# Right halves of four row tiles: two-by-two products of 256 features in place of full products of 512

## The chip, the core and the metric

The kernel runs on one core of a Trainium2 chip. The metric is device time in microseconds (us). Three runs of the kernel before took 358.38, 361.06 and 360.46 us, so the median is 360.46.

A core has a matrix engine (TensorE, PE in the profile), a vector engine (VectorE, DVE), a scalar engine (ScalarE, ACT), a general engine (GpSimd, POOL) and a queue engine that issues transfers (SyncE, SP). Each engine takes its own instructions in order and waits on semaphores for the others.

## The reference

Two layers follow each other on x of 2048 rows and 1024 features. Everything is float32.

```
attn = (w1.T @ w2.T) * sparse_mask                 # 1024 x 1024, a band and two stripes near it
y    = gelu(x @ attn + b2)
x    = layernorm(x + y)
w_l  = lut4[o, code of 4 bits], w_h = lut8[o, code of 8 bits]
y    = where(norm(x) > 64, x @ w_h.T, x @ w_l.T) + bias
x    = layernorm(x + y)
```

The first einsum multiplies each row of x by the masked product of the two weights. The rows of a normalized x have a norm near 32, so the kernel computes only the 4-bit case and counts the rows that would need the other; were there any, a general path would run behind it. It doesn't run with these inputs.

## The kernel before

**Tiles.** The rows are 16 tiles of 128 rows, and each x tile stays in SBUF. `attn` is kept as a band of at most 268 columns for each block of 128 input features. `attention(n)` copies the bias into a PSUM tile (ACT, L526), runs 10 matmuls with the transposed tile as the stationary side (L532), takes Gelu (ACT, L557), adds it to x with a row sum (DVE, L561), takes the sum of squares (ACT, `stats`, L380), r on POOL (L382, L383), and, later, the normalization (DVE, L387). The closures for the later step are kept in a list that `now()` works off.

**Second layer.** `wT` holds the 4-bit weights, transposed, as 8 blocks of 128 input features by 1024 output features; the identity is added to it, so x + y is one product. It is filled while the first tiles go through attention: ACT and POOL make table entries, DVE selects, TensorE transposes and ACT copies (L282). For tiles 0 to 3 (`EARLY`) the second layer is done in two halves of 512 output features: the left one (`ffn_half(n, xT, 0)`) while the weights of the right half are still being made, the right one later, between the attentions of tiles 12 to 15. A half is 8 matmuls of 512 columns (L575), an evacuation with a row sum (`combine`, L587), and at the end `finish_rows`.

**Pairs.** Tiles 4 to 15 go by twos through `ffn_pair`. It has Winograd's form of Strassen's scheme: with the two row tiles as the block rows, and the halves of input and of output features as block columns, seven products of four matmuls do for what is eight otherwise. It needs four weight sums T1 to T4 (`weight_sum`, L636, 128 x 2048 elements each: T1 = B12 - B11, T2 = B22 - T1, T3 = B22 - B12, T4 = B21 - T2) and sums of the transposed row tiles, s1 to s4 (`pair_inputs`: two on DVE, L675 and L676, two on POOL, L678 and L679). The transposed tiles for it are made by `squares`: a transpose of 32 x 32 squares on DVE (L642), a transfer to DRAM (`there`) and four back (`rows`). Products that are shared are accumulated in the same PSUM tile `u`, with DVE reading `u` in between (L705, L712 and `combine`), so TensorE has to wait for that reading before it goes on adding.

**Order.** The list `todo` gives the order in which the steps are written down. PE, ACT and POOL are then ordered by a scheduler with costs of its own. From attention of tile 8 on, DVE keeps the order in which the program is written (`manual_schedule` for DVE, L846). In the list, each right half `m` of 0 to 3 stands ahead of the attention of tile 12 + m, and the weight sum T(m + 1) stands right behind the right half. The pool `last` is opened ahead of tile 10 and takes over the room of the weight preparation, so what lies in it waits for that preparation to end.

Of the kernel before, what the change touches and what calls it, by code (L numbers as in the profile page):

```python
# [9 lines left out]
FP = mybir.dt.float32  # L10
# [22 lines left out]
EARLY = 4  # L33
# [159 lines left out]
def kernel(  # L193
# [21 lines left out]
    with ExitStack() as main:  # L215
# [330 lines left out]
        def now():  # L546
            while later:
                later.pop(0)()
# [24 lines left out]
        def product(ps, xT, h):  # L573
            for k in range(KT):
                nc.tensor.matmul(  # L575
                    out=ps,
                    lhsT=xT[:, k, :],
                    rhs=wT[:, k, ts(h, HALF)],
                    start=(k == 0),
                    stop=(k == KT - 1),  # L580
                )

        sums = const.tile([P, NT, NH], FP, name="sums")

        def combine(n, h, ps, other):

            return nc.vector.scalar_tensor_tensor(  # L587
                x_tiles[n][:, ts(h, HALF)],
                ps,
                1.0,  # L590
                other,
                ALU.mult,
                ALU.add,
                accum_out=sums[:, n, h : h + 1],
            )

        def finish_rows(n):
            y = x_tiles[n]
            total = work.tile([P, 1], FP, tag="total", name="total", bufs=4)
            nc.vector.tensor_tensor(total, sums[:, n, 0:1], sums[:, n, 1:2], ALU.add)  # L600
# [12 lines left out]
        def ffn_half(n, xT, h):  # L613
            ps = ps_mm.tile([P, D], FP, tag="mm", name="mm")
            product(ps[:, :HALF], xT, h)
            now()
            combine(n, h, ps[:, :HALF], bias_bc[:, ts(h, HALF)])
            if h == 1:
                finish_rows(n)

# [10 lines left out]
        def weight_sum(pool, i):  # L631

            plus, minus = sums_of[i]
            weights[i] = pool.tile([P, KH, HALF], FP, tag=f"t{i}", name=f"t{i}")
            minus = weights[minus] if isinstance(minus, int) else minus
            nc.vector.tensor_tensor(weights[i], plus, minus, ALU.subtract)  # L636

        def squares(pool, n):

# [18 lines left out]
        def pair_inputs(pool, n, top, low):  # L658


            def halves(tag):
                both = late.tile([P, KT, P], FP, tag=tag, name="halves")
                return both, both[:, :KH, :], both[:, KH:, :]

            def by_squares(block):
                return block.rearrange("p k (a r) -> p k a r", a=Q)


            side = (n - EARLY) // PAIR % 2
            (a1, a11, a12), (_, s1, s2), (_, s3, s4) = (  # L670
                halves(f"early{2 * i + side}") for i in range(3)
            )
            a22 = pool.tile([P, KH, P], FP, tag="a22", name="a22", bufs=2)
            nc.scalar.copy(by_squares(a1), top)  # L674
            nc.vector.tensor_tensor(by_squares(s1), low[:, :KH], low[:, KH:], ALU.add)  # L675
            nc.vector.tensor_tensor(by_squares(s3), top[:, :KH], low[:, :KH], ALU.subtract)  # L676
            copied = nc.scalar.copy(by_squares(a22), low[:, KH:])
            nc.gpsimd.tensor_tensor(s2, s1, a11, ALU.subtract)  # L678
            nc.gpsimd.tensor_tensor(s4, a12, s2, ALU.subtract)  # L679
            return (a11, a12, a22, s1, s2, s3, s4), copied  # L680

        def ffn_pair(pool, n, blocks, between):

            a11, a12, a22, s1, s2, s3, s4 = blocks
            t1, t2, t3, t4 = (weights[i] for i in range(1, 5))
            u = pool.tile([P, HALF], FP, tag="u", name="u", bufs=2)
            v = pool.tile([P, HALF], FP, tag="v", name="v", bufs=1)
            w = pool.tile([P, HALF], FP, tag="w", name="w", bufs=1)

            def times(ps, a, b, start, stop):  # L690
                for k in range(KH):
                    nc.tensor.matmul(  # L692
                        out=ps,
                        lhsT=a[:, k, :],
                        rhs=b[:, k, :],
                        start=start and k == 0,
                        stop=stop and k == KH - 1,
                        skip_group_check=True,
                    )
# [108 lines left out]
        for m in range(EARLY):  # L808
            todo += [("left", m), ("attention", 4 + m)]
        todo += [("attention", n) for n in range(4 + EARLY, SOON)]  # L810
        for m in range(EARLY):
            todo += [("right", m), ("attention", SOON + m)]
        unpack_after = [("attention", 1), ("left", 0), ("attention", 4), ("left", 1)]
        unpack_after += [("attention", 5), ("left", 2), ("attention", 6), ("left", 3)]

        kept = {}
        rows, blocks = {}, {}

        def prepare_pair(n, part):

# [12 lines left out]
        def prepare(what, n):  # L833
            if what == "attention":
                return first_xT[n] if n < AHEAD else transposed(n, "xT", 2, False)
            if what == "left":
                kept[n] = transposed(n, f"early{n}", 1, True)
            return kept[n]

        ready = prepare(*todo[0])  # L840
        ordered = main.enter_context(ExitStack())
        for i, (what, n) in enumerate(todo):
            if (what, n) == ("left", 0):
                transpose_pending(0)
            if (what, n) == ("attention", 2 * EARLY):
                ordered.enter_context(tc.manual_schedule(engines={mybir.EngineType.DVE}))  # L846
            if (what, n) == ("attention", SOON - 2):
                steps(100)
                transpose_pending(0)
                first_sb.close()  # L850
                last = main.enter_context(tc.tile_pool(name="last", bufs=1, side="right"))
                for m in range(SOON, NT):
                    load_x(last, m)
            xT = ready
            if i + 1 < len(todo):
                ready = prepare(*todo[i + 1])
            if what == "attention":
                if n >= SOON + 1:
                    attention(n, xT, lambda: prepare_pair(EARLY, n - SOON - 1))
                else:  # L860
                    attention(n, xT)
                if n < 2 * EARLY:
# [64 lines left out]
```

## Time and profile before

| what | us |
|---|---|
| median of three runs | 360.46 |
| profiled execution, its own time | 360.45 |
| its span in the profile | 358.7 |
| TensorE busy | 329.9 |
| VectorE busy | 214.5 |
| ScalarE busy | 179.4 |
| GpSimd busy | 90.9 |
| the chain that ended last: share of TensorE | 60% |
| DVE weight sum of 128 x 2048 (L636), each of four | 2.28 |
| POOL sum of 128 x 512 (L678, L679), mean | 1.585, 1.413 |

Times in the profile are counted from the start of the span. An instruction that waits is shown when it starts, with the idle time before it in brackets and what ended that. In the page's slices each digit is the busy share of one fortieth of the span in tenths. A float32 matmul is shown as two instructions, so eight matmuls are x16. The marks in time that the text uses: the four right halves lie between 157.0 and 201.5, the first pair begins at 201.5 and the second at 227.4.

### The profile page before, as it was taken

How to read it: one execution, taken by the hardware profiler on the slowest of the kernel's cores; microseconds unless marked ns; L12 is line 12 of the kernel's file. 1: busy time of each engine (PE TensorE's matmuls, PEld its weight loads, DVE VectorE, ACT ScalarE, POOL GpSimd, SP SyncE). 2: the span in 40 equal slices, each digit the busy share in tenths (PEclk: the TensorE clock that was granted, in tenths of full speed). 3: DMA queues.
4: the chain of work that ended last, by engine and by line, in shares of the span. 5: the costliest groups of instructions: out<-in, count | busy, mean ns of one | idle time of the engine just before them, and what ended most of it. 6: DMA issues, size and time to landing. Idle time of an engine off the chain costs nothing.

```text
span 358.7 us, 3719 instructions
## 1 busy us (share of the span) xinstructions
PE 329.9 (92%) x1228; PEld 205.7 (57%) x1228; DVE 214.5 (60%) x341; ACT 179.4 (50%) x257; POOL 90.9 (25%) x131
## 2 busy tenths in 40 slices
PE   7799867598999999999999998999999999999990
PEld 7688756495765759966656643443444443444450
DVE  0589898546997885436476853653644535634342
ACT  3795893978958988974346311303214114024020
POOL 1630431425013442312312530401304004004010
PEclk9899998879999999999999999999999999999996
DMA  8999207700000000320264425153554450441103
GB/s 250 320 320 384 80 0 288 298 2 0 0 0 2 1 0 3 126 111 26 79 215 165 140 80 175 58 199 100 199 177 137 188 175 8 189 154 58 58 3 125
DMA packets 28475, 43.90 MB, mean 122 GB/s; under 512 B 7584, under 2 KB 20640, under 8 KB 28448
## 3 DMA queue, kind: packets, MB, share of 16 engines
q1 hardware_dynamic: 26832, 42.66, 34.9%
q10 hardware_dynamic: 1616, 0.93, 0.9%
q8 instruction: 11, 0.18, 0.2%
q14 instruction: 16, 0.13, 0.1%
HBM read 28.90 MB, written 14.68 MB: 122 GB/s over the span
## 4 chain that ended last, share of the span: by engine, by line
PE 60%; ACT 12%; DMA 11%; DVE 8%; issue 3%; POOL 2%; SPq 2%; ACTq 0%; POOLq 0%; DVEq 0%
PE u L692 15%; PE mm L532 12%; PE mm L575 12%; PE w L692 8%; ACT e L322 6%; PE pt L281 5%; PE v L692 4%; PE mm L454 4%; DMA rows<-there 3%; ACT junk L380 2%; DMA q<-in_L_ffn_qweight_dram 2%; DMA x<-in_L_attn_x_dram 2%; DMA there<-squares 1%; DMA w_sb<-in_L_attn_w_dram 1%; SPq L652 1%
## 5 line engine op out<-in xcount | busy, mean ns | idle before, releaser
L532 PE MATMUL mm<-attn,xT 128*128 128x198 f32 (+2 forms) x320 | 62.5, 353 | 6.9 <-ACT mm L526 6.9
L380 ACT ACTIVATE junk<-x,nm 128x1024 bf16<-128x1024 f32 x31 | 35.7, 1151 | 59.7 <-DVE nm L377 57.3
L532 PEld LDWEIGHTS mm<-attn,xT 128*128 128x128 f32 x320 | 54.8, 197 | 14.6 <-ACT mm L526 7.6
L322 ACT ACTIVATE e<-v,lt,diff 128x1024 f32<-128x1024 uint8 x48 | 56.8, 1243 | 12.6 <-DVE v L297 11.0
L575 PE MATMUL mm<-wT,xT 128*128 128x512 f32 x128 | 56.4, 593 | 1.0 <-ACT wT L282 1.0
L326 POOL TENSOR_SCALAR root<-v,diff,lt 128x1024 f32<-128x1024 uint8 x16 | 31.3, 1965 | 57.9 <-DVE v L297 26.2
L692 PE MATMUL u<-t,halves 128*128 128x512 f32 x96 | 43.3, 593 | 1.0 <-DVE x L712 1.0
L575 PEld LDWEIGHTS mm<-wT,xT 128*128 128x128 f32 x128 | 23.7, 190 | 28.1 <-issue 26.1
L382 POOL TENSOR_SCALAR r<-ss 128x1 f32<-128x1 f32 x31 | 10.4, 334 | 108.8 <-ACT junk L380 108.6
L674 ACT COPY halves<-rows 128x1024 f32<-128x1024 f32 x6 | 6.3, 1048 | 55.4 <-DMA rows<-there 55.4
L454 PE MATMUL mm<-w2T,w_sb 128*128 128x268 f32 (+1 forms) x128 | 30.8, 391 | 2.2 <-ACT w2T L282 2.2
L692 PEld LDWEIGHTS u<-t,halves 128*128 128x128 f32 x96 | 18.2, 190 | 24.3 <-issue 22.5
L678 POOL TENSOR_TENSOR halves<-halves 128x512 f32<-128x512 f32 x6 | 9.5, 1585 | 84.5 <-DVE halves L675 68.3
L642 DVE STREAM_TRANSPOSE squares<-x 128x1024 f32<-128x1024 f32 x12 | 24.3, 2029 | 11.0 <-DMA there<-squares 11.0
L387 DVE TENSOR_SCALAR x<-x,nm,r 128x1024 f32<-128x1024 f32 x16 | 13.0, 813 | 29.0 <-POOL r L383 29.0
L330 DVE COPY_PREDICATED root<-v,e 128x1024 f32<-128x1024 uint8 x16 | 23.3, 1457 | 8.0 <-POOL root L326 4.6
L454 PEld LDWEIGHTS mm<-w2T,w_sb 128*128 128x128 f32 x128 | 23.8, 197 | 6.2 <-ACT w2T L282 2.7
L281 PE MATMUL pt<-ident,x 128*128 128x128 f32 x160 | 21.8, 281 | 4.0 <-DVE x L387 4.0
L561 DVE SCALAR_TENSOR_TENSOR x<-z,x 128x1024 f32<-128x1024 f32 x16 | 21.4, 1335 | 6.2 <-ACT z L557 6.2
L329 DVE COPY_PREDICATED e<-v,e 128x1024 f32<-128x1024 uint8 x16 | 21.3, 1329 | 3.5 <-ACT e L322 3.5
L281 PEld LDWEIGHTS pt<-ident,x 128*128 128x128 f32 x160 | 19.4, 152 | 5.9 <-DVE x L387 4.3
L282 ACT COPY xT<-pt 128x512 f32<-128x512 f32 x40 | 21.4, 591 | 2.3 <-PE pt L281 2.3
(93 smaller groups left out, 438.5 us busy)
## 6 DMA issues: line engine op xcount, KB each, us to landing
x<-in_L_attn_x_dram SPq DMA_DIRECT2D x16, 512.0 KB, 7.4
out_dram<-o SPq DMA_DIRECT2D x14, 512.0 KB, 2.6
there<-squares SPq DMA_DIRECT2D x12, 512.0 KB, 3.1
rows<-there SPq DMA_DIRECT2D x48, 128.0 KB, 2.9
w_raw<-in_L_attn_w_dram SPq DMA_DIRECT2D x8, 512.0 KB, 6.8
w_sb<-in_L_attn_w_dram SPq DMA_DIRECT2D x3, 1024.0 KB, 6.9
w_sb<-in_L_attn_w_dram SPq DMA_DIRECT2D x2, 512.0 KB, 7.2
x<-_L_attn_sparse_mask_dram SPq DMA_DIRECT2D x2, 413.0 KB, 3.7
```

Source lines behind the costliest of these rows:

```text
L281: nc.tensor.transpose(pt[:, j, :], block(g * (HALF // P) + j), ident)
L282: done = nc.scalar.copy(dst[:, g * (HALF // P) : (g + 1) * (HALF // P), :], pt)
L322: nc.scalar.activation(entry[j], plane(0), AF.Identity, scale=d_k, bias=l_k)
L326: nc.gpsimd.tensor_scalar(entry[j], plane(0), d_k, l_k, ALU.mult, ALU.add)
L330: nc.vector.copy_predicated(root, plane(1), entry[1])
L380: nc.scalar.activation(junk, u, AF.Square, bias=nm, accum_out=ss)
L454: part = nc.tensor.matmul(out=ps[:, : hi - lo], lhsT=w1_sb[s][:, k, :], rhs=w2T[:, k, lo:hi], start=(k == 0), stop=(k == KT - 1),)
L532: nc.tensor.matmul(out=ps[:, a:b], lhsT=xT[:, s, :], rhs=attn[:, s, a - lo : b - lo], start=False, stop=hi == D or (h == 0 and window(s + ...
L561: nc.vector.scalar_tensor_tensor(xt, z, 1.0, xt, ALU.mult, ALU.add, accum_out=total)
L575: nc.tensor.matmul(out=ps, lhsT=xT[:, k, :], rhs=wT[:, k, ts(h, HALF)], start=(k == 0), stop=(k == KT - 1),)
L642: nc.vector.transpose(out=t, in_=x_tiles[n].rearrange("t (c j k) -> t c k j", c=Q, k=KT))
L692: nc.tensor.matmul(out=ps, lhsT=a[:, k, :], rhs=b[:, k, :], start=start and k == 0, stop=stop and k == KH - 1, skip_group_check=True,)
```

## The change

The right halves of tiles 0 to 3 are no longer computed tile by tile. Tiles 0 and 1, and tiles 2 and 3, form a pair each, and the right half of 512 output features is cut in two of 256. So `ffn_rights` does seven products of four matmuls of 256 columns for two tiles; `u` and `w` take tiles of the transposes' PSUM pool, and `v` one of `ps_mm`.

- It needs four weight sums of its own, of 128 x 1024 elements (`right_weight_sums`, on DVE, written behind attention 11). They lie in the room that T3 and T4 get later.
- It needs the sums s1 to s4 of the kept transposed tiles (`early_blocks`, two on DVE and two on POOL for each pair, written behind attention 10).
- The order becomes: rights of tiles 0 and 1, attention 12, attention 13, rights of tiles 2 and 3, attention 14, attention 15.
- The weight sums of the pairs T1 and T3 move to POOL. T1 is written behind attention 12, T2 and T3 behind attention 14, T4 behind attention 15.
- `squares` for tiles 4 and 5 stand in attentions 12 and 13, and the first `pair_inputs` in attention 14.
- The row sums have three parts for tiles 0 to 3, added by a reduction. The tags of `pair_inputs` are dealt out anew.

```diff
-        sums = const.tile([P, NT, NH], FP, name="sums")
+        sums = const.tile([P, NT, 3], FP, name="sums")
...
+            if n < EARLY:
+                nc.vector.tensor_reduce(total, sums[:, n, :], AX.X, ALU.add)
+            else:
+                nc.vector.tensor_tensor(total, sums[:, n, 0:1], sums[:, n, 1:2], ALU.add)
...
-            nc.vector.tensor_tensor(weights[i], plus, minus, ALU.subtract)
+
+            engine = nc.gpsimd if i % 2 else nc.vector
+            engine.tensor_tensor(weights[i], plus, minus, ALU.subtract)
+
+        R = HALF // 2
+        r11, r12 = wT[:, :KH, HALF : HALF + R], wT[:, :KH, HALF + R :]
+        r21, r22 = wT[:, KH:, HALF : HALF + R], wT[:, KH:, HALF + R :]
...
+            t1, t2, t3, t4 = (right_weights[i] for i in range(1, 5))
+            nc.vector.tensor_tensor(t1, r12, r11, ALU.subtract)
+            nc.vector.tensor_tensor(t2, r22, t1, ALU.subtract)
+            nc.vector.tensor_tensor(t3, r22, r12, ALU.subtract)
+            nc.vector.tensor_tensor(t4, r21, t2, ALU.subtract)
...
+        def early_blocks(pool, n):
+
+            a11, a12 = kept[n][:, :KH, :], kept[n][:, KH:, :]
+            a21, a22 = kept[n + 1][:, :KH, :], kept[n + 1][:, KH:, :]
+            both = late.tile([P, KT, P], FP, tag=f"early{EARLY + n // PAIR}", name="halves")
+            s1, s2 = both[:, :KH, :], both[:, KH:, :]
+            s4 = pool.tile([P, KH, P], FP, tag="a22", name="s4", bufs=2)
+            nc.vector.tensor_tensor(s1, a21, a22, ALU.add)
+            nc.vector.tensor_tensor(a21, a11, a21, ALU.subtract)
+            nc.gpsimd.tensor_tensor(s2, s1, a11, ALU.subtract)
+            nc.gpsimd.tensor_tensor(s4, a12, s2, ALU.subtract)
+            blocks[n] = a11, a12, a22, s1, s2, a21, s4
...
+        def ffn_rights(n):
...
+            times(u, a11, r11, True, False)
+            nc.vector.tensor_tensor(y11, u, left, ALU.add)
+            times(w, s1, t1, True, False)
+            nc.vector.tensor_tensor(y22, w, right, ALU.add)
+            times(u, s2, t2, False, False)
+            nc.vector.tensor_tensor(y12, u, right, ALU.add)
+            times(w, s4, r22, False, True)
+            combine(n, 3, w, y12, R)
+            times(u, s3, t3, False, False)
+            combine(n + 1, 3, u, y22, R)
+            now()
+            times(v, a12, r21, True, True)
+            combine(n, 2, v, y11, R)
+            finish_rows(n)
+            times(u, a22, t4, False, True)
+            combine(n + 1, 2, u, left, R)
+            now()
+            finish_rows(n + 1)
...
-        for m in range(EARLY):
-            todo += [("right", m), ("attention", SOON + m)]
+        for m in range(0, EARLY, PAIR):
+            todo += [("rights", m), ("attention", SOON + m), ("attention", SOON + m + 1)]
...
-                if n >= SOON + 1:
-                    attention(n, xT, lambda: prepare_pair(EARLY, n - SOON - 1))
+                if SOON <= n <= SOON + PAIR:
+                    attention(n, xT, lambda: prepare_pair(EARLY, n - SOON))
...
+                if n == SOON - 2:
+                    for m in range(0, EARLY, PAIR):
+                        early_blocks(last, m)
+                if n == SOON - 1:
+                    now()
+                    right_weight_sums(last)
+                for i in {SOON: (1,), SOON + 2: (2, 3), SOON + 3: (4,)}.get(n, ()):
+                    weight_sum(last, i)
+            elif what == "left":
+                ffn_left(n, xT)
             else:
-                ffn_half(n, xT, 0 if what == "left" else 1)
-                if what == "right":
-                    weight_sum(last, n + 1)
-                    now()
+                ffn_rights(n)
```

More of the change, by code (lines that the diff above doesn't have):

```diff
@@ L581, in product, with combine @@
                 )
-        sums = const.tile([P, NT, NH], FP, name="sums")
-        def combine(n, h, ps, other):
+        sums = const.tile([P, NT, 3], FP, name="sums")
+        def combine(n, h, ps, other, width=HALF):
+            i = h if width == HALF else h - 1
             return nc.vector.scalar_tensor_tensor(
-                x_tiles[n][:, ts(h, HALF)],
+                x_tiles[n][:, ts(h, width)],
                 ps,
@@ L593, in combine @@
                 ALU.add,
-                accum_out=sums[:, n, h : h + 1],
+                accum_out=sums[:, n, i : i + 1],
             )
@@ L599, in finish_rows @@
             total = work.tile([P, 1], FP, tag="total", name="total", bufs=4)
-            nc.vector.tensor_tensor(total, sums[:, n, 0:1], sums[:, n, 1:2], ALU.add)
+            if n < EARLY:
+                nc.vector.tensor_reduce(total, sums[:, n, :], AX.X, ALU.add)
+            else:
+                nc.vector.tensor_tensor(total, sums[:, n, 0:1], sums[:, n, 1:2], ALU.add)
             nm, r, _ = stats(y, total)
@@ L611, in finish_rows, with ffn_left @@
             later.append(rest)
-        def ffn_half(n, xT, h):
+        def ffn_left(n, xT):
             ps = ps_mm.tile([P, D], FP, tag="mm", name="mm")
-            product(ps[:, :HALF], xT, h)
+            product(ps[:, :HALF], xT, 0)
             now()
-            combine(n, h, ps[:, :HALF], bias_bc[:, ts(h, HALF)])
-            if h == 1:
-                finish_rows(n)
+            combine(n, 0, ps[:, :HALF], bias_bc[:, :HALF])
         KH = KT // 2
@@ L635, in weight_sum, with right_weight_sums @@
             minus = weights[minus] if isinstance(minus, int) else minus
-            nc.vector.tensor_tensor(weights[i], plus, minus, ALU.subtract)
+            engine = nc.gpsimd if i % 2 else nc.vector
[3 more added lines that the diff above has]
+        r21, r22 = wT[:, KH:, HALF : HALF + R], wT[:, KH:, HALF + R :]
+        right_weights = {}
+        def right_weight_sums(pool):
+            for j in (3, 4):
+                t = pool.tile([P, KH, HALF], FP, tag=f"t{j}", name=f"t{j}")
+                for i in range(2):
+                    right_weights[2 * (j - 3) + i + 1] = t.rearrange("p k (i n) -> p (k i) n", i=2)[
+                        :, i * KH : (i + 1) * KH, :
+                    ]
+            t1, t2, t3, t4 = (right_weights[i] for i in range(1, 5))
[3 more added lines that the diff above has]
+            nc.vector.tensor_tensor(t4, r21, t2, ALU.subtract)
@@ new lines @@
+        kept = {}
+        rows, blocks = {}, {}
+        def early_blocks(pool, n):
[9 more added lines that the diff above has]
+            blocks[n] = a11, a12, a22, s1, s2, a21, s4
@@ new lines, in times @@
+        def times(ps, a, b, start, stop):
+            for k in range(KH):
+                done = nc.tensor.matmul(
+                    out=ps,
+                    lhsT=a[:, k, :],
+                    rhs=b[:, k, :],
+                    start=start and k == 0,
+                    stop=stop and k == KH - 1,
+                    skip_group_check=True,
+                )
+            return done
+        def ffn_rights(n):
+            a11, a12, a22, s1, s2, s3, s4 = blocks[n]
+            t1, t2, t3, t4 = (right_weights[i] for i in range(1, 5))
+            u, w = (
+                ps_tr.tile([P, HALF // P, P], FP, tag="tr", name=name).rearrange(
+                    "p j c -> p (j c)"
+                )[:, :R]
+                for name in "uw"
+            )
+            v = ps_mm.tile([P, D], FP, tag="mm", name="mm")[:, :R]
+            left, right = bias_bc[:, HALF : HALF + R], bias_bc[:, HALF + R :]
+            y11, y12 = x_tiles[n][:, HALF : HALF + R], x_tiles[n][:, HALF + R :]
+            y22 = x_tiles[n + 1][:, HALF + R :]
+            times(u, a11, r11, True, False)
[16 more added lines that the diff above has]
+            finish_rows(n + 1)
@@ L670, in pair_inputs @@
             (a1, a11, a12), (_, s1, s2), (_, s3, s4) = (
-                halves(f"early{2 * i + side}") for i in range(3)
+                halves(f"early{i}") for i in ((0, 1, EARLY), (2, 3, EARLY + 1))[side]
             )
@@ L688, in ffn_pair @@
             w = pool.tile([P, HALF], FP, tag="w", name="w", bufs=1)
[L690 to L699, printed above, removed]
             left, right = bias_bc[:, :HALF], bias_bc[:, HALF:]
@@ L810 @@
         todo += [("attention", n) for n in range(4 + EARLY, SOON)]
-        for m in range(EARLY):
-            todo += [("right", m), ("attention", SOON + m)]
+        for m in range(0, EARLY, PAIR):
+            todo += [("rights", m), ("attention", SOON + m), ("attention", SOON + m + 1)]
         unpack_after = [("attention", 1), ("left", 0), ("attention", 4), ("left", 1)]
         unpack_after += [("attention", 5), ("left", 2), ("attention", 6), ("left", 3)]
-        kept = {}
-        rows, blocks = {}, {}
         def prepare_pair(n, part):
@@ L837, in prepare @@
                 kept[n] = transposed(n, f"early{n}", 1, True)
-            return kept[n]
+            return kept.get(n)
         ready = prepare(*todo[0])
```

## The prediction

> **What bounds the kernel now.** The page's busy times and slices come first, then the stretches of the affected stage, then the timeline of single instructions there.
>
> ```profile
> PE 329.9 (92%) x1228; PEld 205.7 (57%) x1228; DVE 214.5 (60%) x341; ACT 179.4 (50%) x257; POOL 90.9 (25%) x131
> ...
> PE   7799867598999999999999998999999999999990
> ```
>
> TensorE is busy throughout from the eleventh slice on. The stretches of the affected stage say the same:
>
> ```profile
> 157.00:201.50 44.50, 44.50 (x170) 27.97 (x169) 28.37 (x42) 21.95 (x33) 12.04 (x26) 1.00 0.33 110
> 201.50:227.40 25.90, 24.56 (x58) 10.50 (x57) 14.87 (x22) 4.91 (x7) 8.03 (x9) 1.00 0.35 116
> ```
>
> After the length the columns are busy PE, weight load, DVE, ACT and POOL. In 157.0 to 201.5, where the four right halves stand between tiles 12 to 15, TensorE has no gap at full clock; DVE works 28.4 of 44.5 us. In the first pair (201.5 to 227.4) TensorE already loses 1.34 us to DVE. From 227.4 to 350 the pairs run at TensorE's pace, so a shift at 227.4 goes to the end whole. So every product removed counts, as long as DVE, which works in a fixed order, isn't late.
>
> **What is removed.** In the chain that ended last, in order of time, a step of the stage is a right half, an attention and a tile's transposes:
>
> ```profile
> 168.54 6.87 PE mm L575 x16
> 175.41 3.60 PE mm L532 x20
> 179.01 0.87 PE pt L281 x8
> ```
>
> Four right halves of eight matmuls of 512 columns (each two passes, so x16) are 27.5 us. What comes is 14 products of four matmuls of 256 columns. The last pair has that shape in the timeline:
>
> ```profile
> 346.69 1.89 PE L762 MATMUL w<-t,a 128*128 128x256 f32 x8
> ...
> 348.42 1.89 PE L762 MATMUL v<-t,a 128*128 128x256 f32 x8
> ```
>
> From one start to the next 1.73 us: 14 x 1.73 = 24.2. TensorE gains 3.3 us. Four weight sums of 2.28 on DVE become two there and two on POOL, and DVE gets four of 1024 elements (half of 2.28: 1.15 each), four block sums of 512 (0.69 each), and 14 evacuations of 256 (0.42 by the L770 rows, 5.9) for four of 512 (2.8). DVE's balance: -4.6 + 4.6 + 2.8 + 3.1 = +5.9 us. Amounts alone would fit into its idle 16 us; the order decides.
>
> **How POOL and DVE get along.** Three rows of the first pair:
>
> ```profile
> 203.46 0.69 DVE L676 TENSOR_TENSOR halves<-rows 128x512 f32<-128x512 f32 x1
> 203.68 1.59 POOL L678 TENSOR_TENSOR halves<-halves 128x512 f32<-128x512 f32 x1 [1.58 <-DVE halves L675]
> 204.06 2.29 DVE L561 SCALAR_TENSOR_TENSOR x<-z,x 128x1024 f32<-128x1024 f32 x1
> 205.35 2.13 POOL L679 TENSOR_TENSOR halves<-halves 128x512 f32<-128x512 f32 x1
> ```
>
> L561 takes 1.22 as a median; here it takes 2.29 and ends 1.08 after POOL's first sum ends (205.27). POOL's second sum takes 1.27 alone and here 2.13: it ends 1.2 after L561. So sums in SBUF on the two engines exclude each other, each waiting for the other's end; reads of PSUM and the 32-square transposes aren't held. The same shows at 166.64, where POOL's L382 (0.19) takes 0.80 and ends with DVE's weight sum.
>
> **A weight sum on POOL** (2048 elements): no row. From 1.27 for 512, less a start of about 0.15 paid once, 4 x 1.12 + 0.15 = 4.6 us; four times the slower row (1.585) is 6.3. The Trainium skill (GPSIMD Engine Reference, 3.1 and 4.1) measured 4.5 us for this add against 2.29 on VectorE, whose row here is 2.28, and says to keep elementwise sums on VectorE. By amount alone the move frees DVE 2 x 2.28; by the exclusion it holds DVE's SBUF work twice for 4.6. I take 4.6; 6.3 would add about 3.4 us (each of the two is paid once on the chain).
>
> **The order, worked through.** The built program shows the order on each engine. The first sum does not stand where it is written (behind tile 12): nothing else orders POOL, and it comes behind tile 8's r. It starts when the third of four wT copies ends (147.36 to 149.41: about 148.9) and ends at 153.5.
>
> *To the pair's second product.* Tile 9's r, taken at 150.62 now, waits till 153.5; DVE's normalization of tile 9 starts at 154.4 (151.48 now) and holds L561 of tile 10, which stands behind it, till 155.2 (153.83); Square of tile 10 starts at 156.8, Gelu of tile 11 at 158.0, then two xT copies and a bias copy (0.5, 0.5, 1.0): tile 12's attention can start at 161.0. TensorE has had two products since 157.04 and is free at 160.5: 0.5 lost. Meanwhile DVE has the block sums of both pairs in front of tile 10's normalization. In turns with POOL's s2 and s4 (4 x 0.65 and 2 x 1.1) this lasts to 161.5, with r and 0.8 to 162.5, L561 of tile 11 to 163.7, POOL's second s2 and s4 to 166.1, r to 167.0, normalization to 167.7, first right weight sum to 168.9. TensorE has the second product (S1 T1) behind eight of the ten matmuls of tile 12 and is there at 163.8: **5.3 us** idle.
>
> *To the second rights' third product.* From 169.1 TensorE has 24.6 us: products 1.72 x 8 = 13.8, attention 0.8 + 0.8 + 2.8 + 3.6, transposes 2.6, waits 0.2. It stands at 193.7 before S2 T2, which needs U read by DVE. DVE first has: mean of row tile 0 at 179.6; a round trip mean, Square, r, normalization of 2.5 (L380 1.25, L382 to L383 0.85, hand-overs) for tiles 0, 1 and 12, and with the work of each 182.9, 186.6, transpose of tile 4 188.6, L561 189.8, 193.1, transpose of tile 5 195.1, L561 196.3, U at 196.9: **3.2 us** idle. Now such round trips lie beside a weight sum or a whole product. TensorE reaches the first 512 pair at 207.6 instead of 201.5.
>
> *The first 512 pair.* The second POOL sum holds DVE from 199.5 to 204.1 (tile 13's normalization). Then row tile 2's mean 205.6, its output 208.7, row tile 3's 212.4 (two round trips), L675 and L676 213.6, L561 of tile 14 beside POOL 215.7, T2 behind POOL's s4 218.9, r and normalization 220.4, L561 of tile 15 221.6, T4 224.1, U read 224.75. TensorE has u, v, w (3 x 3.43) till 218.0: **6.7 us** idle. Four products (13.7) and two more waits, one on the transpose of tile 7 (1.5) and one on U's last read, since the product V no longer stands between (1.0), make 240.9 for 227.4. SP's transfers are no part of this: from a transpose's end to usable rows it takes 7.05 us (211.61 to 218.66), so tile 4's are there at 195.7 and tile 5's at 202.2, needed at 207 and 212; an output frees the one o tile in 2.6, as fast as the next r comes; mask loads pass into free time. The third sums column and TENSOR_REDUCE (0.19 for 0.16) cost nothing.
>
> **The clock.** This trace shows a price of idling:
>
> ```profile
> 56.24 5.33 PE L532 MATMUL mm<-attn,xT 128*128 128x198 f32 x20 [5.49 <-ACT mm L526]
> 62.28 3.76 PE L532 MATMUL mm<-attn,xT 128*128 128x198 f32 x20
> ```
>
> The same work took 1.6 longer behind 5.49 us of idling (granted clock 0.64 in 55 to 58). Behind 4.04 us at 66.9 it was 0.50 for 70 to 76. The Trainium skill (TensorE: Matmul & The Clock Gate, Part 1) lets the clock fall to half after an idle window of 3.4 us: by it the waits of 5.3 and 6.7 cost clock and that of 3.2 may not; by the row 1.6 each, 2.7 at most. Behind the second, DVE's waits swallow most of it. I take 1.6 in all, zero and 3.5 as ends.
>
> **Sum.** Idling grows by 0.5 + 5.3 + 3.2 + 6.7 + 2.5 - 1.3 (the first pair's now) = 16.9, products shrink by 3.3: 13.6 later at the second pair, and with the clock 15.2. The profiled execution took 360.45 (its span of 358.7 and 1.75 around it), the median of the runs is 360.46: about 375.5 us.
>
> **Rivals.** *Products only:* DVE's order has slack and TensorE keeps its stretch without a gap: 360.45 - 3.3 = 357.1. For it: DVE idles 16 of 44.5 us. Against: it decides from the point where the first right weight sum is ready by 163.8, and three normalizations (two with a round trip), two L561 and eight block sums on two engines stand before it: 0.05. *A draw:* the waits eat just the gain, 357 to 364; the first wait alone is larger: 0.05. *No exclusion:* the two engines only slow each other a little. Without turn-taking the chain to S1 T1 is 2 us shorter and the first pair's 2, and the clock is spared: about 9.6, 370; against it stand the rows at 203 to 207; 0.25, with 367 to 372. *The forecast:* 0.58, 371 to 381. *Longer POOL sums, clock lost twice:* 360.45 + 13.6 + 3.4 + 3.5 is 381: 0.07.
>
> The range of 367 to 381 leaves out the first two and the last. Under 1% (3.6 us) either way a measurement of this kernel hardly tells from nothing: faster 0.05, same 0.05, slower 0.90.
>
> **What would show it.** After: POOL's 2048-element sum near 149 with 4.6 us, and r of tile 9 behind it; an idle of about 5 us on TensorE before S1 T1, released by DVE's first right weight sum, of 3 before the second pair's S2 T2, of 6 to 7 before the first 512 pair's S2 T2; the pairs from the second on with 24 to 25 us each as now; granted clock below 1 near 169. I am wrong if DVE reaches the right weight sums before 164, or POOL's sum is short, or DVE's SBUF work goes on beside it.

## The result, and the profile after

The changed kernel takes 379.73 us (median of four runs, 378.29 to 380.12), against 359.55 for the kernel before in runs beside it: ratio 1.055, 95% interval 1.050 to 1.061. It is slower, inside the range forecast and 4.2 us above the number. The profiled execution took 378.29 us, with a span of 376.5. The page of the changed kernel, its busy times and two rows of its slices (TensorE, and the granted clock in tenths):

```profile
PE 332.0 (88%) x1275; PEld 216.8 (58%) x1276; DVE 222.7 (59%) x361; ACT 179.5 (48%) x257; POOL 106.5 (28%) x137
...
PE   7799849689999999949968958999999999999991
...
PEclk9999978899999999978998996999999999999998
```

TensorE's row now has three dents (slices 18, 21 to 22 and 24 to 25), where before it was full there but for one 8, and the clock's row has dips there too. The first starts of the products concerned, from the timeline of TensorE (start, duration, what it is, in brackets the idle time ahead of it and what ended that):

```profile
166.99 3.78 PE L680 MATMUL w<-t,halves 128*128 128x256 f32 x8 [5.48 <-DVE t L657]
198.64 3.36 PE L680 MATMUL u<-t,halves 128*128 128x256 f32 x8 [4.63 <-DVE x L705]
227.28 6.60 PE L680 MATMUL u<-t,halves 128*128 128x512 f32 x8 [5.91 <-POOL r L383]
241.63 3.67 PE L680 MATMUL u<-t,a 128*128 128x512 f32 x8 [0.88 <-DVE x L588]
245.14 3.60 PE L680 MATMUL u<-wT,halves 128*128 128x512 f32 x8
```

These are S1 T1 of the first rights, S2 T2 of the second, and S2 T2 of the first 512 pair. Each waits for DVE: for the first right weight sum (L657), for a read of U (L705), and for a read of U again (L779, which ended at 227.13; the profile names the POOL instruction that ended beside it). The durations tell a second thing: four matmuls of 256 columns take 1.89 elsewhere and 3.78 and 3.36 here, and those of 512 take 6.60 for 3.60. The stretches show why (half clock, below, is a granted clock of about 0.5). After the length the columns are busy PE, weight load, DVE, ACT and POOL; the third figure from the end is the granted clock:

```profile
161.50:167.00 5.50, 0.02 (x2) 0.01 (x1) 2.22 (x6) 1.24 (x2) 3.95 (x6) 0.81 0.00 0
167.00:170.50 3.50, 3.50 (x8) 2.74 (x9) 3.50 (x4) 0.00 (x0) 0.00 (x0) 0.50 0.00 0
174.90:194.00 19.10, 19.10 (x102) 16.82 (x100) 7.46 (x19) 7.58 (x13) 2.13 (x6) 1.00 0.34 123
198.60:202.00 3.40, 3.36 (x9) 2.71 (x10) 0.22 (x1) 3.37 (x5) 1.13 (x4) 0.57 0.41 133
227.30:233.70 6.40, 6.40 (x8) 2.66 (x9) 4.24 (x4) 0.00 (x0) 0.73 (x2) 0.54 0.21 83
```

Behind each wait TensorE works at about half clock. Stretch length times the missing share gives 1.75 + 1.46 + 2.94, with 0.9 more in the stretches that follow the first two (170.5 to 174.9 at 0.86, 202 to 206 at 0.94): 7.0 us of clock. The whole stage adds up, from the attentions of tiles 10 and 11 (148.97 before, 146.60 after) to the second pair of 512 (227.40, 245.14). It is 20.1 us longer. The waits are 0.15 (ahead of tile 12's attention, for ACT's copy of the bias) + 5.48 + 4.63 + 5.91 + 0.88, less the 1.34 that the stage had: 15.7. Where nothing waits, a product starts about 0.17 before the row of the one ahead ends; three more waits lose that three times, 0.5. Products -3.3, clock 7.0; together 19.9. The stage began 2.4 us earlier in this execution. That lead is there by 85 us, where the two kernels do the same work (in the first 20 us the clock was 0.91 before and 1.00 here). It does not come with the change: the first product of 512 columns starts at 85.49 before and at 83.09 here, but at 85.29 and 85.35 in two variants of the changed kernel ("weights_first", "free_sums_on_dve").

### The profile page after: what moved, and what is told of

The parts are those of the page before. It is cut to its first block, busy times and chain, and to the rows that moved or that the text cites. A ratio compares the mean times of both kernels' runs of the same rounds, so it can differ in the third digit from the quotient of the medians.

```text
span 376.5 us, 3849 instructions
## 1 busy us (share of the span) xinstructions
PE 332.0 (88%) x1275; PEld 216.8 (58%) x1276; DVE 222.7 (59%) x361; ACT 179.5 (48%) x257; POOL 106.5 (28%) x137
## 4 chain that ended last, share of the span: by engine, by line
PE 54%; DVE 15%; ACT 10%; DMA 7%; POOL 6%; issue 5%; SPq 1%; POOLq 0%; DVEq 0%; ACTq 0%
PE u L680 22%; PE w L680 12%; PE mm L532 6%; PE v L680 4%; PE mm L575 4%; PE pt L281 3%; ACT junk L380 3%; DVE x L561 3%; ACT e L322 3%; DVE root L331 2%; DMA w_raw<-in_L_attn_w_dram 2%; DMA out_dram<-o 2%; DMA x<-in_L_attn_x_dram 2%; ACT xT L282 2%; DVE e L329 2%
## 5 line engine op out<-in xcount | busy, mean ns | idle before, releaser
L680 PE MATMUL u<-t,halves 128*128 128x512 f32 (+1 forms) x112 | 51.4, 606 | 10.5 <-POOL r L383 5.9
L680 PEld LDWEIGHTS u<-t,halves 128*128 128x128 f32 x112 | 22.9, 207 | 36.4 <-issue 29.0
L680 PE MATMUL w<-t,halves 128*128 128x512 f32 (+1 forms) x64 | 27.2, 573 | 5.5 <-DVE t L657 5.5
L454 PE MATMUL mm<-w2T,w_sb 128*128 128x268 f32 (+1 forms) x128 | 29.1, 376 | 1.2 <-ACT w2T L282 1.1
L575 PE MATMUL mm<-wT,xT 128*128 128x512 f32 x64 | 28.2, 594 | 1.0 <-ACT wT L282 1.0
L454 PEld LDWEIGHTS mm<-w2T,w_sb 128*128 128x128 f32 x128 | 22.8, 189 | 4.7 <-ACT w2T L282 1.7
L680 PEld LDWEIGHTS w<-t,halves 128*128 128x128 f32 x64 | 13.2, 208 | 18.1 <-issue 11.2
L561 DVE SCALAR_TENSOR_TENSOR x<-z,x 128x1024 f32<-128x1024 f32 x16 | 21.4, 1336 | 3.8 <-ACT z L557 3.8
L281 PEld LDWEIGHTS pt<-ident,x 128*128 128x128 f32 x160 | 20.2, 156 | 5.7 <-DVE x L387 3.7
```

What stands on the lines that cost most here:

```text
L281: nc.tensor.transpose(pt[:, j, :], block(g * (HALF // P) + j), ident)
L454: part = nc.tensor.matmul(out=ps[:, : hi - lo], lhsT=w1_sb[s][:, k, :], rhs=w2T[:, k, lo:hi], start=(k == 0), stop=(k == KT - 1),)
L561: nc.vector.scalar_tensor_tensor(xt, z, 1.0, xt, ALU.mult, ALU.add, accum_out=total)
L575: nc.tensor.matmul(out=ps, lhsT=xT[:, k, :], rhs=wT[:, k, ts(h, HALF)], start=(k == 0), stop=(k == KT - 1),)
L680: done = nc.tensor.matmul(out=ps, lhsT=a[:, k, :], rhs=b[:, k, :], start=start and k == 0, stop=stop and k == KH - 1, skip_group_check=True,)
```

## The experiments

The theory at the outset: DVE's fixed order, with its round trips over ACT and POOL before each normalization, reaches the sums and reads too late. The rivals: the sums on POOL with turn-taking are the cause; single sums stand too late; the clock is a matter of its own. All times are medians; the kernel before took 359.0 to 359.3 in these comparisons.

| kernel | us | ratio to before (95%) | long waits, in order |
|---|---|---|---|
| changed | 379.73 | 1.050 to 1.061 | 5.48, 4.63, 5.91 |
| sums_on_dve | 380.00 | 1.053 to 1.061 | 4.54, 5.44, 7.65 |
| all_on_dve | 377.98 | 1.048 to 1.058 | 2.71, 5.72, 7.66 |
| weights_first | 377.78 | 1.044 to 1.055 | 1.27 and 4.99, 2.61, 6.46 |
| pair_sums_moved | 378.83 | 1.050 to 1.060 | 5.48, 5.59, 2.51 and 2.54 |
| filled | 376.31 | 1.043 to 1.051 | 1.83 and 1.96, 0.84, 0.26 |
| free | 369.96 | 1.026 to 1.033 | 6.00, 3.29, 0.35 |
| free_sums_on_dve | 365.34 | 1.013 to 1.020 | 1.68 and 0.36, 3.30, 0.36 |
| begun_early | 357.87 | 0.995 to 0.999 | 0.35, 1.32, 0.89, 0.69 |
| before_free | 356.36 | 0.990 to 0.994 | 0.52 |
| pool_only | 361.25 | 1.003 to 1.008 | 1.22 |

### The pairs' weight sums back on DVE

```diff
-            engine = nc.gpsimd if i % 2 else nc.vector
+            engine = nc.vector
```

> All four weight sums of the pairs are on DVE again, all else as in the changed kernel. My theory (DVE's order of writing, with a round trip over ACT and POOL before each normalization, makes TensorE wait; POOL's sums only shift that): the three long waits become about 4.2, 3.9 and 7.3 us instead of 5.5, 4.6 and 5.9, their sum stays, and the time is 379.5 us (377.5 to 381.5). Rival (the sums on POOL are the cause, since they hold DVE for 4.5 us each): two such holds go, DVE gets 2 x 2.28 back, some 4 to 5 us of waiting go and part of the lost clock: about 374 us.

380.0 us: no gain. The waits were 4.54, 5.44 and 7.65. So POOL's two long sums are not what makes the change slow in this order: with them gone, DVE's own two further sums of 2.28 stand in the order, and the waits sum to 17.6 for 16.0.

### Nothing of the kind on POOL before the first pair

```diff
-            engine = nc.gpsimd if i % 2 else nc.vector
+            engine = nc.vector
...
-            nc.gpsimd.tensor_tensor(s2, s1, a11, ALU.subtract)
-            nc.gpsimd.tensor_tensor(s4, a12, s2, ALU.subtract)
+            nc.vector.tensor_tensor(s2, s1, a11, ALU.subtract)
+            nc.vector.tensor_tensor(s4, a12, s2, ALU.subtract)
```

> No sum of more than one column is on POOL before the first pair: the weight sums and also s2 and s4 of the early tiles are on DVE. My theory (DVE's order and its round trips): what the two engines no longer take turns for, DVE works off itself; waits of about 2.9, 4.8 and 7.3 us, 379 us (377 to 381). Rival (turn-taking of DVE and POOL is the cause): the 3.4 us by which the working with turn-taking was above the one without go, and some clock with them: 374 to 376 us.

378.0 us, 1.8 below the changed kernel, inside what the order theory gave and outside the rival's. The first wait halves, and the second and third grow. Even behind the wait of 2.71 TensorE was at half clock (3.25 for 1.89, granted 0.59):

```profile
164.79 3.25 PE L680 MATMUL w<-t,halves 128*128 128x256 f32 x8 [2.71 <-DVE t L657]
```

### The right weight sums first

```diff
                 if n == SOON - 2:
+                    right_weight_sums(last)
                     for m in range(0, EARLY, PAIR):
                         early_blocks(last, m)
                 if n == SOON - 1:
                     now()
-                    right_weight_sums(last)
```

> The four weight sums of the right halves stand ahead of the block sums and of the normalization of tile 10 in DVE's order. My theory (the order as a whole is late, not this sum): the wait before S1 T1 falls from 5.5 to about 1.3 us, and one of about 4.7 us appears at the next product, S2 T2, which waits for DVE reading U, which still stands behind the normalization of tile 11; the second and third waits stay: 379.5 us (377.5 to 381.5). Rival (the right weight sums written too late are the cause of the first wait): 5.5 us of waiting and 1.8 us of half clock behind it go: about 372.5 us.

TensorE's timeline of this kernel:

```profile
161.73 1.99 PE L680 MATMUL w<-t,halves 128*128 128x256 f32 x8 [1.27 <-DVE halves L672]
173.41 3.75 PE L680 MATMUL u<-t,halves 128*128 128x256 f32 x8 [4.99 <-DVE x L705]
199.56 1.97 PE L680 MATMUL u<-t,halves 128*128 128x256 f32 x8 [2.61 <-DVE x L705]
227.06 6.66 PE L680 MATMUL u<-t,halves 128*128 128x512 f32 x8 [6.46 <-POOL r L383]
```

The wait for the sum fell to 1.27 and a wait for the read of U took its place, as expected. The time is 377.8, 2.0 below the changed kernel and at the edge of the expectation; that came from the second wait, which was 2.61 and had no half clock behind it. Why that one differs is taken up below.

### T2 and T4 elsewhere

```diff
-                for i in {SOON: (1,), SOON + 2: (2, 3), SOON + 3: (4,)}.get(n, ()):
+                for i in {SOON: (1, 2), SOON + 2: (3,)}.get(n, ()):
...
             nc.vector.tensor_tensor(y11, u, left, ALU.add)
+            if n == EARLY:
+                weight_sum(last, 4)
             now()
             between(0)
```

> The changed kernel with T2 written behind T1, after the attention of tile 12, and T4 behind DVE's first read of U in the first pair of 512. My theory (the order as a whole is late, not these sums): the third wait of 5.9 us becomes two of about 2.7 and 3.0 us, the second of them before S4 B22, since W's read now stands behind T4 and the normalization of tile 15; no half clock or less behind two short waits: 377.5 us (375.5 to 380). Rival (T2 and T4 standing ahead of U's read are the cause of the third wait): 5.5 us of waiting and 2.9 us of half clock go, about 371.5 us.

378.8 us. The third wait became two, 2.51 and 2.54, with no half clock behind them (granted 1.00). The second wait rose by 1.0 to 5.59: 0.3 of it because an output landed later (taken up below), 0.6 because T2 now stands ahead of the second rights. The rest of T2's 2.28 falls into DVE's wait for the next r. What is taken out of one place in the order comes back, in part, in another.

### DVE's order left to the scheduler

```diff
-                ordered.enter_context(tc.manual_schedule(engines={mybir.EngineType.DVE}))
+                pass
```

> The changed kernel with DVE's order left to the scheduler too, as for the other engines (the line that keeps the order of writing on DVE from the attention of tile 8 on is left out); the same instructions. My theory (the fixed order with its round trips is the cause): reads of U and the sums move into the time in which DVE waits for r; the third wait falls from 5.9 to about 1.7 us in two parts, the first two stay near 5.8 and 3.4 since POOL's sums still stand in them: 7.5 us of waiting and some 3 us of half clock less, 369 to 372 us. Rival (amounts and turn-taking, not the order): within 2 us of the changed kernel, 378 to 381 us.

370.0 us, 9.8 below the changed kernel with the same instructions. The third wait is down to 0.35 and the clock there is full:

```profile
168.91 3.78 PE L680 MATMUL u<-t,halves 128*128 128x256 f32 x8 [6.00 <-DVE x L705]
195.52 2.43 PE L680 MATMUL u<-t,halves 128*128 128x256 f32 x8 [3.29 <-DVE x L705]
224.56 3.67 PE L680 MATMUL w<-wT,halves 128*128 128x512 f32 x8 [0.35 <-DVE x L783]
```

So the order of writing, with the same work on DVE, is worth 9.8 of the 20.2 us lost, about half. The other engines' orders, which the scheduler makes, come out anew with DVE's (TensorE takes S1 T1 ahead of tile 12's attention here), so the 9.8 belongs to the new schedule as a whole. The same edit in the kernel before was the control:

> The kernel before with DVE's order left to the scheduler, the same instructions. My theory: the waits of the first pair on reads of U and W (0.3 and 1.0 us) go, and little else, 357.5 us (356 to 359.5). Rival (the order written by hand is the better one as long as the right halves leave it slack): 360 us or more.

356.4 us, ratio 0.992: the order written by hand costs 2.6 us there and 9.8 here.

### The order freed, and the sums on DVE

This kernel has the edits of "free" and "sums_on_dve" together.

> The changed kernel with DVE's order left to the scheduler and all four weight sums of the pairs on DVE. My theory: now that the order gives way, POOL's two sums of 4.5 us are what holds DVE; without them the first wait falls from 6.0 to about 2.2 us in two parts and the clock stays up there, the second stays near 3.5; 4 us less than with the order freed alone, and some clock: 364 to 366 us. Rival (POOL's sums are covered in the freed order): 369 to 371 us.

365.3 us. In the fixed order the sums on POOL cost nothing (380.0 without them); once the order gives way they cost 4.6 us. TensorE's first wait shrinks from 6.00 to 1.68 and 0.36. Each cause was hidden behind the other. The second wait is as long as in "free" (3.29 there), but the product behind it ran at full clock (1.99; granted 1.00 from 193.5 to 201), where in "free" it took 2.43 and the clock fell to 0.61 in 198 to 201:

```profile
168.32 1.99 PE L680 MATMUL u<-t,halves 128*128 128x256 f32 x8 [1.68 <-DVE x L705]
193.51 1.99 PE L680 MATMUL u<-t,halves 128*128 128x256 f32 x8 [3.30 <-DVE x L705]
```

### The products begun early

The edits of "free" and "all_on_dve", and the products U and W of both rights with DVE's reads of them in a function of their own, called ahead of a normalization (only the calls are shown):

```diff
+                if n == SOON + 1:
+                    begin_rights(PAIR)
                 if SOON <= n <= SOON + PAIR:
...
-                if n == SOON - 2:
-                    for m in range(0, EARLY, PAIR):
-                        early_blocks(last, m)
                 if n == SOON - 1:
-                    now()
                     right_weight_sums(last)
+                    early_blocks(last, 0)
+                    begin_rights(0)
+                    now()
+                    early_blocks(last, PAIR)
```

> The changed kernel with DVE's order left to the scheduler, no sums of more than one column on POOL before the first pair, and the first two products of each pair of right halves, with DVE's reads of them, written ahead of the normalizations that held them up. My theory: the waits are then about 0.9, 1.8, 1.4 and 0.7 us, each too short to cost clock, and the 3.3 us of removed products come through: 357 us (355.5 to 359). Rival (the products were never worth it, since their 14 reads of 256 columns on DVE make new waits of the same sum): 360 us or more.

357.9 us, ratio 0.997 (0.995 to 0.999): faster than the kernel before, and 1.5 us slower than "before_free" in the same comparison. Waits of 0.35, 1.32, 0.89 and 0.69 are left in the stage, with full clock. That is 3.25 for the 3.3 that the products save. The rest lies earlier: the freed order has moved six block sums of 0.7 on DVE into the preparation of the weights (100 to 132), and two waits there are longer. That the sums make them so is not shown by a run of its own. TensorE's timeline of this kernel:

```profile
118.33 3.86 PE L532 MATMUL mm<-attn,xT 128*128 128x198 f32 x20 [1.74 <-ACT mm L526]
133.13 3.86 PE L532 MATMUL mm<-attn,xT 128*128 128x198 f32 x20 [1.46 <-ACT mm L526]
```

In "before_free" the same two waits are 0.67 and 0.79, 1.74 less. So here the products are worth about what their reads and sums cost. Both kernels beat the one before; the one that gains more does it without the change.

### One part alone: two sums on POOL in the kernel before

```diff
-            nc.vector.tensor_tensor(weights[i], plus, minus, ALU.subtract)
+            engine = nc.gpsimd if i % 2 else nc.vector
+            engine.tensor_tensor(weights[i], plus, minus, ALU.subtract)
```

> The kernel before with one part of the change alone: T1 and T3 of the pairs' weight sums on POOL. My theory (in an order with slack, POOL's sums of 4.5 us hold DVE but hardly TensorE): a wait of about 1.3 us more, 360.3 us (359 to 362). Rival (each sum on POOL costs its 4.5 us of held DVE work on the path): 364 us or more.

361.25 for 358.97 beside it: 2.3 us more, ratio 1.005 (1.003 to 1.008). One new wait of 1.22 is in the trace, ahead of the attention of tile 12. The part alone is cheap where the order has slack, though a little dearer than expected.

### How DVE and POOL get along

```diff
             nc.vector.tensor_tensor(y22, w, right, ALU.add)
+            if n > EARLY:
+                nc.gpsimd.tensor_tensor(
+                    attn[:, :, :256], wT[:, :, :256], wT[:, :, 256:512], ALU.subtract
+                )
             between(1)
```

> The kernel before with one more subtraction of 128 x 2048 on POOL in each pair from the second on, from wT into the band of attn, which is no longer used then; nobody reads it. It measures how the two engines get along. My theory (sums in SBUF on the two engines exclude each other): a DVE sum in SBUF that falls into the 4.5 us is held to its end; DVE's reads of PSUM (0.69 us) and its 32-square transposes (2.0 us) keep their durations within 0.1 us. Rival (the engines only share bandwidth): all of DVE's operations in it are longer by the same small share, none by over 0.5 us.

The scheduler put all five sums close together, between 201 and 231. The lines of DVE and POOL in that window of the probe:

```profile
201.66 9.43 POOL L711 TENSOR_TENSOR attn<-wT 128x2048 f32<-128x2048 f32 x2
201.73 5.01 DVE L387 TENSOR_SCALAR o<-x,nm,r 128x1024 f32<-128x1024 f32 x1 [0.72 <-POOL r L383]
206.66 4.98 DVE L675 TENSOR_TENSOR halves<-rows 128x512 f32<-128x512 f32 x1
211.56 0.68 DVE L676 TENSOR_TENSOR halves<-rows 128x512 f32<-128x512 f32 x1
...
225.64 5.04 POOL L711 TENSOR_TENSOR attn<-wT 128x2048 f32<-128x2048 f32 x1
226.18 2.04 DVE L642 STREAM_TRANSPOSE squares<-x 128x1024 f32<-128x1024 f32 x1
228.14 0.66 DVE L709 TENSOR_TENSOR x<-w,bias_bc 128x512 f32<-128x512 f32 x1
```

A normalization of 0.81 takes 5.01 and a sum of 0.69 takes 4.98: each waits for a whole POOL sum to end and then runs. The transpose (2.04) and the read of PSUM (0.66) inside a POOL sum keep their time. This is turn-taking by whole instructions, and the rival of shared bandwidth is out. The Trainium skill (SBUF — State Buffer, "SBUF: two separate sides") says the same of the port pair that the two engines share: an exclusive lock for a whole instruction, taken by a GpSimd operation and by a DVE operation in a two-port mode or, against a GpSimd operation that reads SBUF, with two SBUF inputs. The trace agrees for the sum with two inputs (4.98 for 0.69); in which mode the normalization runs it doesn't tell. The one execution took 377.2 us; most of the 17.9 above the kernel before are two waits of TensorE of about 7 us with slow products behind them (5.84 and 5.73 for 3.60).

### The waits filled with useless products

Products that nobody reads are added ahead of the three that wait.

```diff
             nc.vector.tensor_tensor(y11, u, left, ALU.add)
+            if n == 0:
+                fill(spare, a12, r11, 5)
             times(w, s1, t1, True, False)
             nc.vector.tensor_tensor(y22, w, right, ALU.add)
+            if n == PAIR:
+                fill(spare, a12, r11, 2)
             times(u, s2, t2, False, False)
...
+            if n == EARLY:
+                fill(spare[:, :R], a11, r11, 3)
```

> The changed kernel with useless products of 256 columns (nobody reads them) written ahead of the three products that wait: five groups of four matmuls at the first, two at the second, three at the third, 17.3 us of TensorE's time in all. The attention of tile 12 moves behind the first ones, so that by my working of the order everything stands 3.5 us later than in the changed kernel; no wait is longer than about 2.2 us. My theory (some 7 us of the changed kernel's time are half clock behind its three long waits, and the clock falls only because TensorE idles): that half clock goes, 376 us (374 to 378). Rival (the clock loss is not tied to idling, or is small, and the time is all waiting): 382 us or more.

376.3 us, 3.4 below the changed kernel with 17.3 us more work on TensorE. No wait is longer than 1.96, and the clock in the stage is full (third figure from the end of the stretches):

```profile
157.00:202.00 45.00, 40.37 (x200) 35.10 (x199) 23.70 (x42) 14.87 (x23) 15.28 (x25) 1.00 0.26 88
202.00:245.00 43.00, 42.74 (x151) 26.60 (x150) 26.97 (x42) 12.22 (x18) 15.50 (x19) 1.00 0.28 92
```

The half clock is tied to idling and costs what the stretches say. From the attentions of tiles 10 and 11 to the second pair this kernel takes 96.5 for the 98.5 of the changed one: 17.3 of products more, 12.2 of waits less, 0.2 for one wait fewer, and 7.0 of clock less make the 2.1 measured.

### What the second wait hangs on

It was 4.63 in the changed kernel and 5.44, 5.72, 2.61 and 5.59 in the four variants that keep DVE's written order and fill nothing. The queue and DVE show what goes with it. In the changed kernel, DVE's second output of a row tile waits for the first to leave the one buffer o:

```profile
182.80 0.35 SPq L613 DMA_DIRECT2D out_dram<-o  x1
183.25 0.38 SPq L516 DMA_DIRECT2D x<-_L_attn_sparse_mask_dram  x1
```

```profile
187.76 0.81 DVE L387 TENSOR_SCALAR o<-x,nm,r 128x1024 f32<-128x1024 f32 x1 [4.74 <-DMA out_dram<-o]
```

The output took 4.8 us to land, with a mask load of 413 KB issued 0.45 behind it; before, the three outputs of the stage took 2.6 to 2.9. In "weights_first" the first landed in 2.9 and the wait was 2.61; in "sums_on_dve", "all_on_dve" and "pair_sums_moved" it took 5.0, 4.5 and 5.2, and the waits were 5.44, 5.72 and 5.59. (In these three a weight sum on DVE stands in the stretch too; by the trace of "pair_sums_moved" it adds 0.6.) The mask load stands 0.44 or 0.45 behind the output in all five, and in "filled", where the output landed in 2.9 as well. So the load alone does not make it late; what does stays open, and no run takes the load away or gives o a second buffer.

## Why the prediction was right, and where it was not

**The order decides.** This held. The expectation of where DVE would be late named the three products, and their waits were 5.48, 4.63 and 5.91 for 5.3, 3.2 and 6.7. The run with the order freed gets 9.8 us back with the same instructions. "begun_early" loses nothing any more (357.9) with more work on DVE (225.5 us busy for 222.7). So it is the order, and which engine has the sums, not the amount.

**The first sum on POOL** started at 146.61 and took 4.53 (4.6 taken). The stage is 2.4 earlier here, so that is 149.0 by the old count, for 148.9. The profile names DVE's L561, which ended at 146.57, as what released it; the third wT copy, which the working named, ended at about 146.5, so this trace does not tell the two apart. Tile 9's r came behind it and the normalization started at 152.09 (154.5 for 154.4). The 0.5 lost ahead of tile 12's attention was 0.3.

```profile
146.61 4.53 POOL L640 TENSOR_TENSOR t<-wT 128x2048 f32<-128x2048 f32 x1 [1.13 <-DVE x L561]
151.23 0.19 POOL L382 TENSOR_SCALAR r<-ss 128x1 f32<-128x1 f32 x1
```

**To the pair's second product.** The round trip that the working put there is in the trace of DVE, with 3.21 of idling ahead of the normalization of tile 11 and the sum right behind:

```profile
164.99 0.81 DVE L387 TENSOR_SCALAR x<-x,nm,r 128x1024 f32<-128x1024 f32 x1 [3.21 <-POOL r L383]
165.72 1.22 DVE L657 TENSOR_TENSOR t<-wT 128x1024 f32<-128x1024 f32 x1
```

**To the second rights' third product.** The step "an output frees the one o tile in 2.6, as fast as the next r comes; mask loads pass into free time" failed: the output took 4.8 beside a mask load, and the wait was 4.63 for 3.2.

**The first 512 pair.** T2 was held by POOL (3.17 for 2.28), and a normalization, L561 and T4 stood between it and the read of U, as worked out:

```profile
218.31 3.17 DVE L640 TENSOR_TENSOR t<-wT,t 128x2048 f32<-128x2048 f32 x1
...
224.25 2.28 DVE L640 TENSOR_TENSOR t<-wT,t 128x2048 f32<-128x2048 f32 x1
...
226.44 0.69 DVE L779 TENSOR_TENSOR x<-u,bias_bc 128x512 f32<-128x512 f32 x1
```

The wait was 5.91 for 6.7. Of the two later ones, 1.5 and 1.0, only 0.88 came: S2 T2 ran at half clock for 6.60, and DVE's transpose passed beside it. All in all idling grew by 16.2 for 16.9, and the products gave their 3.3. That the sum comes so near is in part luck: the second wait was 1.4 longer than forecast, the third 0.8 and the later ones 1.6 shorter.

**The clock** is the term that was mis-sized: 1.6 was taken, 3.5 was the upper end, and it was 7.0. The step that failed is the count. The price of 1.6 to 2.7 for a wait, read from the rows of the kernel before, was near, but it was charged once for three waits. The second got nothing by the 3.4 us window of the Trainium skill (TensorE: Matmul & The Clock Gate, Part 1), since it was forecast at 3.2; at its 4.63 that window would have charged it. The third was to be swallowed by DVE's waits. Each of the three cost its own: about 2.4, 1.7 and 2.9. In the third, half clock swallowed one of DVE's waits, not the other way round. The run with filled waits shows that this cost is due to idling.

**What the parts sum to.** Idling 0.7 less than forecast, clock 5.4 more, an early lead of 2.4 that belongs to no step, and 0.5 that rounding leaves (the forecast's own terms make 375.65, not 375.5): 2.8 above 375.5, which is the profiled run's 378.29. The median is 1.4 above that run.

**The rivals.** *Products only* and *a draw* are out by the waits. *No exclusion* is out as a mechanism, by the probe. But the weight I gave to turn-taking was too simple: in the fixed order the sums are no dearer on POOL than on DVE (380.0 against 379.7). They cost 4.6 us only when the order is freed. The mechanism was right. The number that hung on it, about 4 us between a kernel with turn-taking and one without, no run measures: every variant that ends the turn-taking also moves the sums to DVE.

## What to carry to other kernels

Fewer products pay only if the engine that reads them can keep up in its order. Where an engine works in a written order with round trips in it, a late wait can be a symptom: here, moving the one sum that ended the wait moved the wait to the next read, and only another order took it away. Count half clock behind each long wait as a term of its own, in the work that follows. In this stage every wait of 4.5 us or more had it, none of 2.6 or less, and of three between 2.7 and 3.3 two did. And before crediting a restructuring, free the order of the kernel without it: here that alone gained more.

## What had not been expected

- Useless work made the kernel faster: 17.3 us of products on TensorE gave 3.4 us back, since they kept its clock up.
- How little idling it takes to lose the clock: behind 2.71 us ("all_on_dve", first wait) the next product took 3.25 for 1.89, behind 2.61 ("weights_first") 1.97, behind 1.96 ("filled") 1.97. Yet behind 3.30 ("free_sums_on_dve") it took 1.99. So 2.71, shorter than the window of 3.4 named above, was enough, and the longer 3.30 was not; what decides between them stays open.
- A POOL sum of 4.7 us can hold a short DVE operation for nearly all of its length: 5.01 for a normalization of 0.81.
